# Flamingo gated block: values by seven block products, the output projection in one slot, another order at the end

## The chip, the cores and the metric

The kernel runs on one core of one Trainium2 chip. The metric is the device time of one execution in microseconds; three runs were timed, and one more was recorded by the hardware profiler. The engines are called as in the profile: PE is TensorE's matmul stream and PEld its weight loads, DVE is VectorE, ACT ScalarE, POOL GpSimd, SP the queue that issues most DMAs.

## The reference, cut to what matters

There are 8 batches of 512 rows (channels) by 2048 columns (positions). The row-wise layernorm of x gives queries and keys, the context gives values; attention runs inside windows of 128 positions with 8 heads of 32; the result goes through a GELU and an output projection and is added to x with a gate. Then a second layernorm feeds a router of 64 experts per row, whose eight best weights scale the row and mix rows of a bias table.

```python
q = einsum('ed,bdw->bew', Wq, qp) + bq        # qp: layernorm(x), windows of 128
k = einsum('ed,bdw->bew', Wk, qp) + bk
val = einsum('ed,bdw->bew', Wv, vp) + bv      # vp: context, 512 rows in, 256 out
attn = softmax(where(mask > 0, q·k / sqrt(32), -1e9))
o = gelu(attn · val)
x = x + tanh(g_xattn) * (Wo · o + bo) * mask
h = layernorm(x)                              # over the 2048 positions
s = softmax(h · router_weight.T + router_bias)   # 64 experts per row
w = the 8 largest of s per row, 0 elsewhere
x = x + tanh(g_ffn) * (h * sum(w) + w · expert_bias)
```

## The kernel before, in words

All arithmetic is in float32. The positions of a batch are cut in 4 chunks of 512, 32 chunks in all, and a chunk in two pairs of windows. The unit of the main loop (line 755) is one pair, called a slot here: slot `g` belongs to chunk `ch = g // 2`, and is even or odd. Eight slots make a batch; `fin` (line 774) counts them 0 to 7 from the second batch on, because the router of a batch is finished while the next batch runs.

The program is scheduled by hand (line 89): each engine executes its instructions in the order in which the code issues them, and a later instruction waits behind an earlier one that waits. The code's order is therefore the order of each engine's queue.

A slot issues, in this order: `scores` (line 430, query times key for 2 windows and 8 heads in four PSUM banks of the tag `sc`), `weigh` and `weighed` of the pair two slots back (lines 499 and 516, attention times values, emptied by ACT), `maxima` (line 456), `exps` in four quarters on ACT (line 461), `divide` by the row sums in two halves (line 473, DVE reciprocal and POOL multiplication), and between these the eight transposes of the pair before in four `turn`s (line 483, emptied by `turned` on ACT). `queries_and_keys` (line 361) projects half of the next chunk's queries and keys by seven block products of the Strassen-Winograd kind instead of eight; the sums of x blocks it needs come from `sums_of_x` (line 298) on POOL, its additions u4 and q from POOL, the others from DVE. `between(i)` puts turns between the products.

Values: `values` (line 409) computes a pair's values with the context window as stationary operand and 256 columns of `wv_sb` as moving operand, four blocks of 128 rows accumulated; `values_out` (line 420) adds the bias. In the loop each slot makes the values of the next chunk's pair of the same parity.

Output projection: `attend` (line 535) makes 128 of 512 rows for a chunk, with DVE adding the bias and multiplying by the mask, and POOL adding the result to x. Of a chunk's four attends, two (m = 0, 1) are issued at the end of an odd slot (line 928) and two (m = 2, 3) early in the following even slot (line 817). Even slots then transpose the new x (`turn_x`, line 560), odd slots make the router's logits of it (`logits`, line 568).

Router: in slot fin 2 the second layernorm's statistics are aggregated (line 888), in fin 3 the logits are gathered and `choose`d (lines 593, 605), in fin 4 `select` (line 630) finds the eight best, and from then on each slot scales two x blocks (`scale_x`, line 665, POOL) and adds the mix of expert rows (`mix`, line 676: two PE products, two DVE additions, one DMA out). In fin 5 the next batch's first layernorm is aggregated, and its chunk is normed by ACT (line 874).

PSUM has eight banks: four of `sc`, two of `tr` (transposes and `weigh`, line 87) and two of `mm` (all other products, line 88), each tag taken in turn. A product waits until the reader of the tile two before it in its tag is done.

The last two pairs and the end are written out (lines 943 to 1050): attention, values and attends of the last chunks, then the last logits, the expert choice and 8 scalings and mixes.

Of the kernel before, what the change touches and what calls it, by code (L numbers as in the profile page):

```python
# [35 lines left out]
def flamingo_gated_kernel(  # L36
# [81 lines left out]
    def load_mask(ch):  # L118
        t = work.tile([P, CW], F32, tag="mk", name=f"mk_{ch}", bufs=4)
        nc.sync.dma_start(t, masks[ch // NCH, :, columns(ch)].to_broadcast([P, CW]))  # L120
        mks[ch] = t
# [66 lines left out]
    ones = const.tile([P, P], F32, name="ones")  # L188
    nc.vector.memset(ones, 1.0)
# [126 lines left out]
    def mask(ch):  # L316
        m01 = work.tile([P, CW], F32, tag="m01", name=f"m01_{ch}", bufs=1)
        nc.vector.tensor_scalar(m01, mks[ch], 0.0, scale, ALU.is_gt, ALU.mult)
        mneg = work.tile([P, CW], BF16, tag="mneg", name=f"mneg_{ch}")
        nc.vector.tensor_scalar(mneg, m01, 0.0, None, ALU.is_equal)  # L320
        m01s[ch], mnegs[ch] = m01, mneg
        qss[ch] = work.tile([P, NE, CW], F32, tag="qs", name=f"qs_{ch}")
        kss[ch] = work.tile([P, NE, CW], F32, tag="ks", name=f"ks_{ch}")
# [12 lines left out]
    def first_queries_and_keys():  # L336


        parts = [(w, e, product([P, CW], f"pf_{i}_{e}", NE * i + e))
# [21 lines left out]
    def queries_and_keys(ch, e, between):  # L361


        es = slice(e * P, (e + 1) * P)
        x_, t_ = xn[ch], xts[ch]
        q, k = qss[ch][:, e, :], kss[ch][:, e, :]
        bq_, bk_, m01 = bq_sb[:, e : e + 1], bk_sb[:, e : e + 1], m01s[ch]
# [37 lines left out]
        nc.vector.tensor_tensor(k, k, m01, ALU.mult)  # L405
# [14 lines left out]
    def values_out(ch, h):  # L420
# [4 lines left out]
        vTs[ch, h] = vT  # L425

# [89 lines left out]
    def weighed(g):  # L516
        ch, hf = g // NH, g % NH
        if hf == 0:
            os_[ch] = work.tile([P, NE, CW], F32, tag="o", name=f"o_{ch}")
# [15 lines left out]
    def attend(ch, m, cs=whole, r=None):  # L535
# [12 lines left out]
        nc.gpsimd.tensor_tensor(xc, t[:, cs], xc, ALU.add)  # L548
# [116 lines left out]
    def scale_x(b, k, on_act=False):  # L665
        t = experts[b]
        j, mp = k // 2, k % 2
        for m in (2 * mp, 2 * mp + 1):
            xc = xr[b * NCH + j][:, m, :]
            a, d = t["a"][:, m : m + 1], t["d"][:, m : m + 1]  # L670
            if on_act:
                nc.scalar.activation(xc, xc, AF.Identity, bias=d, scale=a)
            else:
                nc.gpsimd.tensor_scalar(xc, xc, a, d, ALU.mult, ALU.add)  # L674

    def mix(b, k):
# [10 lines left out]
        for i in range(2):  # L687
            xc = xr[ch][:, 2 * mp + i, :]
            nc.vector.tensor_tensor(xc, pb[i], xc, ALU.add)  # L689
# [54 lines left out]
    def router_sums():  # L744
        pr = ps_tr.tile([P, E], F32, tag="tr", name="pr")
# [9 lines left out]
    for g in range(NG - NH):  # L755
# [7 lines left out]
        n_pieces = [4, 4, 4, 2, 2][g] if g < 5 else PER  # L763
# [4 lines left out]
        xch = ch - 2 if even and ch >= 2 else None  # L768
        lch = ch - 2 if not even and ch >= 2 else None
        pch = ch - 1 if not even and ch >= 1 else None  # L770

        vals = [] if (nxt, h) == (1, 0) or nxt == last else [(nxt, h)]
# [11 lines left out]


        if even:
            if nxt > 1:
                load_cx(nxt, 1)
            if nxt < last and nxt + 1 >= NCH:
                load_xn(nxt + 1)  # L790
        elif nxt < last:
            load_cx(nxt + 1, 0)
        if even and NCH <= ch - 1:
            load_xr(ch - 1)
# [8 lines left out]

        def read_x(n):

            for b, i in pieces[:n]:
                stats_x(b, i)
                if queue:
                    load_raw(*queue.pop(0))
            del pieces[:n]  # L810

# [3 lines left out]
        if even:  # L815
            if xch is not None:
                for m in (2, 3):
                    attend(xch, m)
                del os_[xch], mks[xch]
            exps(g, 1)  # L820
            exps(g, 2)
            mask(nxt)
            turn_(0)
            turn_(1)
            exps(g, 3)
# [3 lines left out]
            divide(g, 0)  # L829
            if g == 0:  # L830
                load_mask(2)
        else:
            exps(g, 1)
            if lch is not None:
                logits(lch)
                logits_out(lch)
# [12 lines left out]
        def between(i):  # L849
            if even:  # L850
                turn_x_(i)
# [6 lines left out]
            else:  # L858
                turn_(2)
                if pch is not None and nxt < last:  # L860
                    load_mask(nxt + 1)

        queries_and_keys(nxt, h, between)
        if fin == 5 and b4 + 2 < B:
# [5 lines left out]
        divide(g, 1)  # L870
        if not even and nxt < last:

            if (nxt + 1) % NCH == 0:
                norm(nxt + 1)
            sums_of_x(nxt + 1, 0)


        if fin == 4:
            select(b4)
        def stats():  # L880
            if even and xch is not None:
                for m in range(NM):
                    statistics2(xch, m)
            read_x(len(pieces))

        if fin != 4:
            stats()
        if fin == 2:
            aggregate(st2.pop(b4), NCH, f"2_{b4}")


        if even:
            turn_x_(2)
            for c_, h_ in vals:
                values(c_, h_, 0, 0)
                turn_(2)
                values(c_, h_, 1)
            if not vals:
                turn_(2)
            if nxt < last and (nxt + 1) % NCH:  # L900
                norm(nxt + 1, (0, 1))
            for c_, h_ in vals:
                values_out(c_, h_)
            if fin == 4:
                stats()
            turn_x_(3)
# [3 lines left out]
            if nxt < last and (nxt + 1) % NCH:  # L910
                norm(nxt + 1, (2, 3))
            if fin == 4:
# [5 lines left out]
        else:  # L918
# [5 lines left out]
            for c_, h_ in vals:  # L924
                values(c_, h_, 0, 0)
                values(c_, h_, 1)
                values_out(c_, h_)
            if pch is not None:
                for m in (0, 1):
                    attend(pch, m, r=m + 1)  # L930
# [6 lines left out]
        if g == 3:  # L937
            nc.gpsimd.tensor_scalar_mul(eb_sb, eb_sb, tgates[:, 1:2])
        for k in steps:
            mix(mb, k)  # L940


    z, b, h0 = last, B - 1, NG - NH
    load_xr(z - 1)
    scores(h0)
# [5 lines left out]
    for m in (2, 3):  # L951
        attend(z - 2, m)
    for k in (2, 3):
        scale_x(b - 1, k)
    exps(h0, 1)
    divide(h0, 0)
    turn(h0 - 1, 0)
    turned(h0 - 1, 0)
    values(z, 0, 0)
    turn(h0 - 1, 1)  # L960
    turned(h0 - 1, 1)
    values(z, 0, 1)
    values_out(z, 0)
    exps(h0, 2)
    exps(h0, 3)
    divide(h0, 1)
    turn_x(z - 2, 0)
    values(z, 1, 0)
    turn_x(z - 2, 1)
    values(z, 1, 1)  # L970
    values_out(z, 1)
    for m in range(NM):
        statistics2(z - 2, m)
    turn(h0 - 1, 2)
    turned(h0 - 1, 2)
    turn_x(z - 2, 2)
    mix(b - 1, 2)
    turn(h0 - 1, 3)
    turned(h0 - 1, 3)
    turn_x(z - 2, 3)  # L980
    mix(b - 1, 3)
    load_xr(z)

    g = h0 + 1
    scores(g)
    weigh(g - 2)
    weighed(g - 2)
    maxima(g, (0, 1))
    maxima(g, (2, 3))
    logits(z - 2)  # L990
    logits_out(z - 2)
    exps(g, 0)
# [3 lines left out]
    exps(g, 1)  # L996
# [4 lines left out]
    exps(g, 2)  # L1001
    for k in (4, 5, 6, 7):
        scale_x(b - 1, k)
    mix(b - 1, 4)
    weigh(g - 1)
    weighed(g - 1)
    exps(g, 3)
    divide(g, 1)
# [3 lines left out]
    gelu(z - 1)  # L1012
    mix(b - 1, 5)
# [3 lines left out]
    late += [0, 1, 2, 3, None, None]  # L1017
# [3 lines left out]
    mix(b - 1, 6)  # L1021
    for m in range(NM):
        attend(z - 1, m)
    mix(b - 1, 7)
    for k in range(KC):
        attend(z, k)
        turn_x(z - 1, k)

    table_of_exps()
    logits(z - 1)  # L1030
    logits_out(z - 1)
    for m in range(NM):
        statistics2(z - 1, m)
        statistics2(z, m)
    for k in range(KC):
        turn_x(z, k)
    aggregate(st2.pop(b), NCH, f"2_{b}")
    logits(z)
    logits_out(z)
    nmean, rs = refine(f"2_{b}")  # L1040
    experts[b] = {"nmean": nmean, "rs": rs}
    gather(b)
    choose(b)
    choose_exps(b)
    select(b)
    turn_weights(b)
    for k in range(2 * NCH):
        scale_x(b, k, k % 2 == 0)
    for k in range(2 * NCH):
        mix(b, k)  # L1050

# [33 lines left out]
```

## Time and profile before

| what | value |
|---|---|
| median of 3 runs | 1371.4 us (1369.75 to 1372.12) |
| the profiled execution's own time | 1372.72 us |
| its span, first to last instruction | 1370.9 us |
| mean granted PE clock | 0.985 |
| starts of `scores` at slots 14, 15, 16 | 306.62, 326.54, 346.53 us |
| starts of `scores` at slots 19 and 20 (fin 3 and 4) | 406.37 and 427.62 us |
| POOL, `divide` (L477), x128 | 1.909 us each |
| POOL, 128x512 additions (L548, L306 to L311) | 1.27 to 1.30 us each |
| ACT, `turned` (L497), x256 | 0.623 us each |

A row of the groups gives line, engine, operation, output and inputs, count, busy time and mean duration, then the idle time before it with what ended it. PE instructions are pipelined, so their pace is read from the starts of successive rows in the timeline and not from their durations. A float32 product appears as two instructions.

### The profile page before, as it was taken

The numbers are of one execution on the slowest core, as the hardware profiler recorded it, in microseconds if no ns is written. First come the engines' busy times: TensorE is split into PE (matmuls) and PEld (weight loads), VectorE is DVE, ScalarE is ACT, GpSimd is POOL, SyncE is SP. The second block draws the span as 40 slices with busy tenths as digits, with TensorE's granted clock in tenths as the row PEclk, the third lists the DMA queues.
The fourth block names the chain that finished last, engine by engine and source line by source line (L and its number), as shares of the span: only waits on it lengthen the run. The fifth ranks groups of instructions, "written<-read, shape, count | busy, mean of one in ns | idle before, by whom it ended". The sixth has DMA issues, their size and how long they took to land.

```text
span 1370.9 us, 26555 instructions
## 1 busy us (share of the span) xinstructions
PE 1317.3 (96%) x9816; PEld 961.0 (70%) x9816; DVE 912.9 (67%) x1981; ACT 832.0 (61%) x2837; POOL 778.0 (57%) x656
## 2 busy tenths in 40 slices
PE   7899999999999999999999999999999999999984
PEld 4686777777777677767777777776777777776642
DVE  5556665676676766786667767677677766567536
ACT  0565666757656666747665675666675566575533
POOL 3456565555566655557555566655556665556452
PEclk9999999999999999999999999999999999999997
DMA  8432323424434433444442444343444343232213
GB/s 276 133 102 71 101 65 129 131 70 156 153 131 139 161 100 133 147 140 141 151 137 96 146 162 141 129 158 97 139 147 161 109 131 105 75 122 78 104 67 123
DMA packets 109666, 173.32 MB, mean 126 GB/s; under 512 B 9185, under 2 KB 43617, under 8 KB 109409
## 3 DMA queue, kind: packets, MB, share of 16 engines
q1 hardware_dynamic: 105680, 168.32, 37.5%
q10 hardware_dynamic: 3856, 3.32, 0.7%
q8 instruction: 77, 1.26, 0.4%
q14 instruction: 53, 0.43, 0.1%
HBM read 138.06 MB, written 33.55 MB: 125 GB/s over the span
## 4 chain that ended last, share of the span: by engine, by line
PE 84%; DVE 11%; POOL 2%; DMA 1%; issue 1%; ACT 0%; DVEq 0%; POOLq 0%; ACTq 0%
PE qk L378 27%; PE po L539 16%; PE pv L415 13%; PE pt L491 7%; PE pl L574 4%; PE pb L685 4%; PE pa L510 4%; PE sc L447 3%; PE px L563 3%; DVE st L558 3%; DVE st L264 2%; PE sc L438 1%; PE pf L344 1%; DMA cx<-in_ctx 1%; DVE ks L405 1%
## 5 line engine op out<-in xcount | busy, mean ns | idle before, releaser
L477 POOL TENSOR_TENSOR at<-at,rsum 128x1024 f32<-128x1024 f32 x128 | 244.3, 1909 | 289.9 <-DVE rsum L476 255.4
L468 ACT ACTIVATE at<-sc,nmx 128x128 f32<-128x128 f32 x1024 | 365.7, 415 | 16.1 <-DVE nmx L459 16.1
L468 ACT ACTIVATION_READ_ACCUMULATOR at<-sc,nmx 128x1 f32 x1024 | 260.1, 254 | 0.0
L415 PE MATMUL pv<-wv_sb,cx 128*128 128x256 f32 x1024 | 242.6, 386 | 10.2 <-DMA cx<-in_ctx 10.2
L539 PE MATMUL po<-o,wo_sb 128*128 128x512 f32 x512 | 233.8, 599 | 0.0
L415 PEld LDWEIGHTS pv<-wv_sb,cx 128*128 128x128 f32 x1024 | 191.4, 194 | 33.8 <-DMA cx<-in_ctx 10.6
L548 POOL TENSOR_TENSOR xr<-t,xr 128x512 f32<-128x512 f32 x128 | 165.9, 1296 | 79.9 <-DVE t L545 79.5
L497 ACT COPY atT<-pt 128x512 f32<-128x512 f32 x256 | 151.1, 623 | 60.4 <-PE pt L491 60.3
L520 ACT COPY o<-pa 128x512 f32<-128x512 f32 x64 | 37.6, 587 | 243.9 <-PE pa L510 243.9
L459 DVE TENSOR_REDUCE nmx<-sc 128x4 f32<-128x512 f32 x256 | 158.7, 681 | 16.7 <-PE sc L447 16.6
L545 DVE SCALAR_TENSOR_TENSOR t<-po,bo_sb,mk 128x512 f32<-128x512 f32 x128 | 96.1, 751 | 109.5 <-PE po L539 104.6
L491 PEld LDWEIGHTS pt<-ident,at 128*128 128x128 f32 x1024 | 123.3, 142 | 61.8 <-issue 41.5
L539 PEld LDWEIGHTS po<-o,wo_sb 128*128 128x128 f32 x512 | 94.3, 190 | 100.4 <-issue 93.9
L565 ACT COPY x1T<-px 128x512 f32<-128x512 f32 x128 | 74.9, 587 | 139.3 <-PE px L563 136.2
L491 PE MATMUL pt<-ident,at 128*128 128x128 f32 x1024 | 152.2, 277 | 5.8 <-POOL at L477 5.3
L378 PE MATMUL qk<-xt,wq_sb 128*128 128x256 f32 x496 | 129.6, 384 | 4.0 <-DVE u L386 3.9
L378 PE MATMUL qk<-xn,ws 128*128 128x256 f32 x496 | 128.6, 382 | 0.0
L378 PE MATMUL qk<-xn,wk_sb 128*128 128x256 f32 x496 | 127.5, 380 | 0.0
L689 DVE TENSOR_TENSOR xr<-pb,xr 128x512 f32<-128x512 f32 x128 | 81.8, 683 | 36.4 <-PE pb L685 33.4
L674 POOL TENSOR_SCALAR xr<-xr,xa,xd 128x512 f32<-128x512 f32 x120 | 94.4, 798 | 18.6 <-DVE xa L650 18.6
L378 PEld LDWEIGHTS qk<-xn,ws 128*128 128x128 f32 x496 | 94.7, 191 | 13.0
L378 PEld LDWEIGHTS qk<-xn,wk_sb 128*128 128x128 f32 x496 | 89.4, 190 | 9.7
(108 smaller groups left out, 2016.3 us busy)
## 6 DMA issues: line engine op xcount, KB each, us to landing
out_dram<-xr SPq DMA_DIRECT2D x64, 512.0 KB, 3.4
cx<-in_ctx SPq DMA_DIRECT2D x63, 512.0 KB, 5.2
raw<-in_x SPq DMA_DIRECT2D x112, 256.0 KB, 3.4
xn<-in_x SPq DMA_DIRECT2D x28, 1024.0 KB, 7.3
xr<-in_x SPq DMA_DIRECT2D x28, 1024.0 KB, 7.8
mk<-in_mask_Bx1x_ff SPq DMA_DIRECT2D x32, 256.0 KB, 5.3
xr<-in_x SPq DMA_DIRECT2D x8, 256.0 KB, 6.4
xr<-in_x ACTq DMA_DIRECT2D x8, 256.0 KB, 6.9
```

The lines of the kernel that those rows point to most:

```text
L378: nc.tensor.matmul(out_, w_[:, j, es], xb[:, j, :], start=(j == 0), stop=(j == NM // 2 - 1))
L415: nc.tensor.matmul(pv[:, i, :], cx[:, m, i * W : (i + 1) * W], wv_sb[:, m, :], start=(m == 0), stop=(m == NM - 1),)
L459: nc.vector.tensor_reduce(p["nmx"][:, r, :, :], p["sc"][r], AX.X, ALU.max, negate=True)
L468: nc.scalar.activation(p["at"][i][:, h, :], p["sc"][r][:, i, e, :], AF.Exp, bias=p["nmx"][:, r, i, e : e + 1], accum_out=p["rsum"][:, i, h ...
L477: (engine or nc.gpsimd).tensor_tensor(p["at"][i], p["at"][i], rs[:, :, None].to_broadcast([P, H, W]), ALU.mult)
L491: nc.tensor.transpose(pt[:, r, :], p["at"][i][:, e * HR + r, :], ident)
L497: nc.scalar.copy(p["atT"][i][:, e * HR : (e + 1) * HR, :], p.pop("pt"))
L539: nc.tensor.matmul(po[:, cs], wo_sb[:, e, m * P : (m + 1) * P], os_[ch][:, e, cs], start=(e == 0), stop=(e == NE - 1),)
L545: nc.vector.scalar_tensor_tensor(t[:, cs], po[:, cs], bo_sb[:, m : m + 1], mks[ch][:, cs], ALU.add, ALU.mult)
L548: nc.gpsimd.tensor_tensor(xc, t[:, cs], xc, ALU.add)
L674: nc.gpsimd.tensor_scalar(xc, xc, a, d, ALU.mult, ALU.add)
L689: nc.vector.tensor_tensor(xc, pb[i], xc, ALU.add)
```

## The change

- **Values by seven products.** For chunks 2 to 31 `values_by_seven` replaces `values`: in the even slot of the chunk itself, seven block products with 128 moving columns, in the four `sc` banks. `sums_of_c` makes three sums of context blocks on POOL in the slot's middle, a fourth comes between the products; `sums_of_wv` makes four sums of weights once, in the fourth slot. DVE empties seven products instead of two. Both halves of a chunk's context are loaded in the odd slot before.
- **Output projection.** All four attends of a chunk are issued at the end of the odd slot, the first two in banks sc0 and sc1. The logits of an odd slot are those of the chunk whose x was turned in the even slot before, with its statistics behind them (not in fin 3; there they come in fin 2, after the values).
- **Order in the slots.** In even slots the turns 0 and 1 follow `weigh` directly; `exps` 3 and `mask` move between the products; `divide` 0 follows the projections and `divide` 1 the values; reading raw x pieces moves to the slot's end. The first five slots read 2, 2, 4, 4, 4 pieces instead of 4, 4, 4, 2, 2. The mask's load moves to the even slot's start, with 3 buffers instead of 4; tag `o` has 1 buffer.
- **The end.** Scores of the last pair are issued between the last values' products; the last divide runs on DVE; the last chunk's attends add on DVE; scalings and mixes 4 to 7 of the batch before move behind the last logits; the last scalings are split over DVE, POOL and ACT, and four of the last additions go to POOL, with ACT emptying PSUM for them.

```diff
+    def sums_of_c(ch):
+        a11, a21, a22 = cxs[ch, 0][:, d1, :], cxs[ch, 1][:, d1, :], cxs[ch, 1][:, d2, :]
...
+        nc.gpsimd.tensor_tensor(t1, a21, a22, ALU.add)
+        nc.gpsimd.tensor_tensor(t2, t1, a11, ALU.subtract)
+        nc.gpsimd.tensor_tensor(a21, a11, a21, ALU.subtract)
+
+    def values_by_seven(ch, between, banks=range(4)):
...
+        def pair(*ops):
+            pv = product([P, len(ops), NPP, P], f"pv_{ch}_{len(banks)}", banks.pop(0))
+            for n, (a, w_) in enumerate(ops):
+                for i in range(NPP):
+                    for j in range(NM // 2):
+                        nc.tensor.matmul(
+                            pv[:, n, i, :], a[:, j, i * W : (i + 1) * W], w_[:, j, :],
+                            start=(j == 0), stop=(j == NM // 2 - 1),
+                        )
+            return [pv[:, n, :, :] for n in range(len(ops))]
+
+        bias = [bv_sb[:, None, e].to_broadcast([P, NPP, P]) for e in (e1, e2)]
+        p1, p6 = pair((c0[:, d1, :], v11), (t2, wt2))
+        nc.vector.tensor_tensor(s1, p1, bias[0], ALU.add)
+        nc.vector.tensor_tensor(u2, p6, s1, ALU.add)
+
+        nc.gpsimd.tensor_tensor(t2, c0[:, d2, :], t2, ALU.subtract)
+        between(0)
+        p2, p5 = pair((c0[:, d2, :], v21), (t1, v12))
+        nc.vector.tensor_tensor(vt[0][:, :, e1], p2, s1, ALU.add)
+        nc.vector.tensor_tensor(s5, p5, bias[1], ALU.add)
+        nc.gpsimd.tensor_tensor(u4, u2, s5, ALU.add)
+        between(1)
+        p7, p3 = pair((c1_[:, d1, :], wt3), (t2, v22))
...
+        nc.vector.tensor_tensor(u3, p7, u2, ALU.add)
+        nc.vector.tensor_tensor(vt[0][:, :, e2], p3, u4, ALU.add)
+        nc.gpsimd.tensor_tensor(vt[1][:, :, e2], u3, s5, ALU.add)
+        between(2)
+        (p4,) = pair((c1_[:, d2, :], wt4))
+        nc.vector.tensor_tensor(vt[1][:, :, e1], p4, u3, ALU.add)
...
         exps(g, 0)
         if even:
-            if xch is not None:
-                for m in (2, 3):
-                    attend(xch, m)
-                del os_[xch], mks[xch]
+            turn_(0)
+            turn_(1)
             exps(g, 1)
             exps(g, 2)
-            mask(nxt)
-            turn_(0)
-            turn_(1)
-            exps(g, 3)
+            if vch is not None:
+                sums_of_c(vch)
             if fin != 4:
                 for k in steps:
                     scale_x(mb, k)
-            divide(g, 0)
...
+            if xch is not None:
+                logits(xch)
+                logits_out(xch)
+                if fin != 3:
+                    for m in range(NM):
+                        statistics2(xch, m)
...
         queries_and_keys(nxt, h, between)
+        if even:
+            divide(g, 0)
...
+            if vch is not None:
+                values_by_seven(vch, between_values)
...
+            divide(g, 1)
+            if fin == 2:
+                for m in range(NM):
+                    statistics2(xch, m)
+                aggregate(st2.pop(b4), NCH, f"2_{b4}")
             if fin == 4:
                 turn_weights(b4)
             turn_(3)
             if nxt < last and (nxt + 1) % NCH:
                 norm(nxt + 1, (2, 3))
+            read_x(len(pieces))
...
         if g == 3:
             nc.gpsimd.tensor_scalar_mul(eb_sb, eb_sb, tgates[:, 1:2])
+            sums_of_wv()
         for k in steps:
             mix(mb, k)
+        if pch is not None:
+            for m in range(NM):
+                attend(pch, m, r=m if m < 2 else None)
+            del os_[pch], mks[pch]
```

## The prediction

> **What bounds the kernel now.** I read the page first (engine shares, chain, groups by shape), then the waits of TensorE in the loop, then the timelines of single slots. One turn of the main loop is a slot; two slots, even and odd, serve one chunk, eight serve a batch, and I count them 0 to 7 by the code's `fin`.
>
> ```profile
> PE 1317.3 (96%) x9816; PEld 961.0 (70%) x9816; DVE 912.9 (67%) x1981; ACT 832.0 (61%) x2837; POOL 778.0 (57%) x656
> ...
> PE 84%; DVE 11%; POOL 2%; DMA 1%; issue 1%; ACT 0%; DVEq 0%; POOLq 0%; ACTq 0%
> PE qk L378 27%; PE po L539 16%; PE pv L415 13%; PE pt L491 7%; PE pl L574 4%; PE pb L685 4%; PE pa L510 4%; PE sc L447 3%; PE px L563 3%; DVE st L558 3%; DVE st L264 2%; PE sc L438 1%; PE pf L344 1%; DMA cx<-in_ctx 1%; DVE ks L405 1%
> ```
>
> The chain that ended last is TensorE work. Its waits between 100 and 1270 us say how little it stands still; the largest:
>
> ```profile
> PE pl L574 <- DVE xr L689: 3.6, 11, 0.3
> PE sc L438 <- DVE t L545: 2.6, 5, 0.5
> PE px L563 <- POOL xr L548: 2.5, 2, 1.4
> ```
>
> A chunk takes 39.9 us (scores start at 306.62, 326.54, 346.53) and TensorE has no gap in it. So whatever is taken from TensorE is won, and any new wait of TensorE is lost in full. The first line names a wait to remember: the logits product takes the PSUM bank from which VectorE still adds the expert mix.
>
> **The skill.** "TensorE: Matmul & The Clock Gate", LDWEIGHTS section: a load costs its columns over 1.2 GHz, about 107 ns for 128, and fp32 has no fast load. The trace agrees: products with 64 moving columns come every 0.112 us (rows L747). The same page, HAM oscillation: an idle TensorE is put on half clock. The trace shows it after less idle time than the page names (below). "SBUF — State Buffer", Who interferes with whom: a VectorE `tensor_scalar` and a GpSimd instruction hold a shared port for a whole instruction. L320 takes 1.30 us in the mean against 0.43 at 46.64 us, where GpSimd is quiet. It agrees.
>
> **The change, part by part.**
>
> ```profile
> 320.62 1.89 PE L415 MATMUL pv<-wv_sb,cx 128*128 128x256 f32 x8
> 322.35 0.60 PE L491 MATMUL pt<-ident,at 128*128 128x128 f32 x4
> 322.78 1.89 PE L415 MATMUL pv<-wv_sb,cx 128*128 128x256 f32 x8
> ```
>
> (1) Values. From start to start, eight instructions of 256 columns take 1.73 us (0.216 each), four transposes, 128 weights and 128 columns, 0.43 (0.109). A chunk now has 32 of the first: 6.92 us. After it has 7 products x 2 windows x 2 blocks x 2 passes = 56 of 128 columns. No row has this shape as an ordinary fp32 product; the nearest are 0.109 (transposes) and 0.112 (L747, where the load sets the pace), the slowest relative 0.126 (four L447 side by side). I take 0.111: 6.2 us, so -0.7 a chunk, 30 chunks: **-21** (-25 to +4).
>
> (2) The even slot loses its two attends between `weigh` and the turns. The second turn then needs the PSUM buffer that ScalarE is still emptying. The kernel's third slot, at 71 us, has no attends and so this order already; the third line is the usual pace:
>
> ```profile
> 73.36 1.43 PE L491 MATMUL pt<-ident,at 128*128 128x128 f32 x8
> 74.14 0.42 PEld L491 LDWEIGHTS pt<-ident,at 128*128 128x128 f32 x4 [0.35 <-ACT o L520]
> ...
> 312.38 1.04 PE L491 MATMUL pt<-ident,at 128*128 128x128 f32 x8
> ```
>
> The second turn starts 0.34 us late. 29 even slots: **+10**.
>
> (3) GpSimd gets 3 sums of 1.24, one of 1.26 and two of 0.73 a chunk, 6.4 us on 24 (60% to 76%), and all four attend additions come in a row, ahead of these. I follow its queue. In the odd slot its second divide starts at 12.99 (339.53 - 326.54), then 1.86, four sums of x 4.95, four additions 4.95: 24.8, with the even slot starting at 20.1, so 4.7 into it. Three sums of c (3.7), two scalings (1.5), about 0.3 for VectorE's mask on the shared port, u4 (0.73): 11.0. Behind u4 VectorE writes k, q, k x mask and the reciprocal (1.6), GpSimd divides (1.9) and makes t2 anew (1.3): 15.85. TensorE wants t2 at 15.65 (scores 1.22, weigh 1.02, turns 1.2, seven products 6.05, two turns of x 0.87, then 1.77 + 0.44 + 1.77 + 0.44 + 0.87). So **+0.2** a chunk (0 to +0.9), 29 times: **+6**. The cover is gone: anything later on GpSimd shows.
>
> (4) VectorE gets seven emptyings of about 0.42 for two of 0.68: +1.6 us a chunk, on 26.5. Regular slots hold that. Slot 2 of a batch does not. Now its statistics lie under the values' matmuls, and still the mix additions are just late:
>
> ```profile
> 408.23 1.27 DVE L689 TENSOR_TENSOR xr<-pb,xr 128x512 f32<-128x512 f32 x2
> ...
> 408.96 1.94 PE L574 MATMUL pl<-x1T,rw_sb 128*64 128x512 f32 x8 [0.30 <-DVE xr L689]
> ```
>
> Afterwards all of it follows the last value product: emptying 0.42, reciprocal 0.12, four statistics 2.37, aggregate 0.83, two raw pieces 1.19, refine 0.83, first addition 0.6, 0.15 of latency: 6.5 us. TensorE meanwhile has a turn 0.44, mix 1.06, scores 1.22, weigh 1.02: 3.7. So the logits of slot 3 wait **2.8**. Behind them queue all turns and projections of that slot.
>
> (5) Slot 4's scalings come behind a divide that now follows the values, so the mix additions, maxima and, in slot 5, the statistics (2.37, moved here) and aggregate (0.83) push VectorE's u2 behind the turn after which TensorE wants its bank: 0.8 at the logits and about 1.2 at the fifth product, **+2.0** (0.7 to 2.6). In slot 5 the norm (four of 0.73 on ScalarE) starts only after the reciprocal, so GpSimd's row of (3) begins 3 us later: slot 6 waits for the additions and for t2, 1.0 to 3.2, taken **+2.5**.
>
> (6) Waits of this length cost again:
>
> ```profile
> 58.82 1.13 PE L378 MATMUL qk<-xt,wq_sb 128*128 128x256 f32 x4 [2.28 <-DVE u L386]
> 59.79 1.52 PE L378 MATMUL qk<-xn,ws 128*128 128x256 f32 x4
> 61.10 1.06 PE L491 MATMUL pt<-ident,at 128*128 128x128 f32 x4
> 61.96 1.84 PE L378 MATMUL qk<-xt,wq_sb 128*128 128x256 f32 x4
> ```
>
> After 2.28 us idle, four products take 1.67 instead of 0.86 for 3.4 us: 1.7 lost. After 1.66 idle (46 us) they did not. I take one such a batch, **+1.7** (0 to 3.4).
>
> A batch so costs 2.8 + 2.0 + 2.5 + 1.7 = 9.0, less the 0.8 that slots 3 and 5 wait or stretch now: +8.2. Seven batches, of which the first and last have about half: 6 x 8.2 = **+49** (22 to 67).
>
> (7) Head, slots counted from the kernel's start. The first two read fewer raw pieces, and their waits of 1.66 and 2.28 and the half clock go: -5. At the end of the fourth, GpSimd scales `eb` (5.4) and makes four sums of wv (2.9) ahead of all four additions: these end 14.3 us into the fifth, where TensorE wants them at 7.3, so 7.0 + 1 (t2) + 3 (clock), against 4.6 lost there now: +7. Together **+2** (-3 to +6).
>
> (8) End. Before, the last scores but one start at 1274.65 and the last logits at 1339.33: 64.7. Afterwards I walk 55: waits of about 5 where ScalarE's exponentials hold the two turn buffers, but divide on VectorE removes the 4.53 us wait at 1312 (behind eight scalings, 6.0), and mixes and scalings move into the expert selection. Two attends (3.5) move ahead of it, so -6. From the last logits on: statistics no longer delay the last sum (-1.8), four mix additions (+1.1) come before the selection and four after it (+2.6), against earlier warm mixes and adds shared out (-3): -1. **-7** (-12 to -2).
>
> (9) At nothing: the mask load waits for the last attend (0.9 into the even slot) and lands 5.3 later, 6.2, before VectorE's 7.6; SP's x and xr loads queue behind it by 0.9 and are used a slot later. Both c loads go out a slot ahead (5.2 to land). Uncovered, each delay would add to (3).
>
> Sum: -21 + 10 + 6 + 49 + 2 - 7 = **+39**. On the profiled execution's 1372.7: 1411.7; the median lies 1.3 below it, so **1410**, slower.
>
> **Rivals.** A, faster: VectorE and GpSimd absorb (3) to (6), as they do now with 67% and 57%; then -21 + 10 - 7 = -18: 1353. For it speaks that TensorE has almost no waits today; against it, 0.30 us at L574, which shows that the slack is used up. It decides if a batch loses under about 3 us. B, the change doesn't do what it says: at 0.126 or more per product, the values save nothing: +25, 1435. Against it, the two nearest rows. C: GpSimd is late by 0.9 in every even slot, +20: 1430. D: only the wait of (4) and half of (5): 1374 to 1385.
>
> **Chances.** Forecast (1385 to 1426) 0.50, A 0.23, no change (within 0.2%, about what a measurement of this kernel can tell) 0.05, D 0.10, B and C 0.12. Slower 0.72, same 0.05, faster 0.23. The range 1357 to 1438 leaves out half of A and the outer part of B and C; the forecast's own is 1385 to 1426.
>
> **What would show it.** Value products 0.111 apart; a 0.34 us wait for L520's successor in even slots; slot 3 lengthened by about 3 us with the logits waiting for VectorE; slot 6 by about 2 waiting for GpSimd; more half-clock stretches. If slot 3 is not over 22 us, (4) is wrong and A likely.

## The result, and the profile after

The changed kernel takes **1440.15 us** (median of 4 runs, 1436.85 to 1444.24) against 1371.67 (4 runs) in the same measurement: ratio 1.050, 95% interval 1.047 to 1.054. Slower, as predicted, but by 68 us instead of 39; 1440.15 lies 14 us beyond the forecast's own 1385 to 1426, and 2 beyond 1438, the upper end of the whole range. The profiled execution took 1437.97, its span 1436.2, which is 65.3 over the span before.

First the page of the changed kernel: busy time by engine, then the chain that ended last.

```profile
PE 1322.2 (92%) x10536; PEld 978.2 (68%) x10536; DVE 965.0 (67%) x2134; ACT 832.5 (58%) x2842; POOL 968.4 (67%) x837
...
PE 53%; POOL 20%; DVE 16%; issue 4%; ACT 4%; DMA 3%; POOLq 0%; SPq 0%; DVEq 0%; ACTq 0%
PE qk L381 17%; PE po L619 8%; PE pv L477 8%; POOL xr L628 5%; PE pt L569 5%; PE pl L654 3%; POOL at L555 3%; DVE st L638 3%; PE pa L588 2%; PE pb L766 2%; POOL xr L755 2%; PE sc L525 2%; PE px L643 2%; ACT xn L283 2%; POOL cx L456 1%
```

TensorE is as busy as before (1322 against 1317), only 65 us more spread out. The chain has passed from TensorE, 84%, to TensorE 53% with GpSimd 20% and VectorE 16%. Which waits made it pass, the list of TensorE's waits over the whole span says (waited for, us in total, times, longest):

```profile
PE pl L654 <- DVE xr L774: 25.5, 13, 3.3
PE pv L477 <- POOL cs L488: 15.9, 14, 1.6
...
PE qk L381 <- DVE u L389: 9.3, 9, 1.3
PE pt L569 <- ACT o L600: 8.3, 31, 3.1
PE pb L766 <- DVE ks L403: 6.6, 6, 1.1
PE px L643 <- POOL xr L628: 5.1, 5, 2.0
PE pb L766 <- DVE xr L774: 4.7, 4, 2.7
```

The first was 3.6 in all before. From start to start of the scores, slot by slot: a regular even slot went from 19.92 to 19.63 us, a regular odd one from 19.99 to 20.31; slot 3 of a batch from 21.25 to 24.55 or 26.18, slot 4 from 20.56 to 20.93, slot 5 from 20.41 to 24.11, slot 6 from 19.92 to 21.49. So the regular chunk costs the same as before, and nearly all is lost in slots 3 to 6.

By stretches of the span. Some work has changed its stretch: chunk 4's values have moved out of the first and chunk 28's into the third, and two attends from the last stretch into the first.

| stretch | before | after | difference |
|---|---|---|---|
| slots 0 to 7 | 144.8 | 149.3 | +4.5 |
| slots 8 to 55 | 971.1 | 1025.6 | +54.6 |
| slots 56 to 61 | 118.3 | 128.7 | +10.4 |
| slot 62 to the end | 96.3 | 90.8 | -5.5 |

Slot 0 itself starts 1.3 later, at 41.8 us. TensorE waits longer for the first loads there (13.0 against 10.2 in all), and this varies: in the runs below slot 0 starts between 38.7 and 41.6.

The worst wait, in slot 3, first VectorE, then TensorE:

```profile
759.37 0.19 DVE L554 RECIPROCAL rsum<-rsum 128x8 f32<-128x8 f32 x1
759.48 2.42 DVE L638 BATCH_NORM_STATS2 st<-xr 128x6 f32<-128x512 f32 x4
761.81 0.61 DVE L242 BATCH_NORM_AGGREGATE mv<-st 128x2 f32<-128x24 f32 x4
...
762.54 1.28 DVE L262 BATCH_NORM_STATS2 st<-raw 128x6 f32<-128x512 f32 x2
...
765.25 1.27 DVE L774 TENSOR_TENSOR xr<-pb,xr 128x512 f32<-128x512 f32 x2
```

```profile
761.63 1.08 PE L588 MATMUL pa<-atT,vT 128*32 128x128 f32 x32
765.98 1.94 PE L654 MATMUL pl<-x1T,rw_sb 128*64 128x512 f32 x8 [3.27 <-DVE xr L774]
```

Statistics, aggregate, raw pieces and refinement all stand between the last value's emptying (759.03) and the mix additions (765.25), and the logits product needs the bank that the first addition frees. VectorE is not busy beyond its means: before 759 it had stood idle for 3.3 us, waiting for value products.

### The profile page after: what moved, and what is told of

It is laid out like the page before. It is cut to its first block, busy times and chain, and to the rows that moved or that the text cites. A ratio compares the mean times of both kernels' runs of the same rounds, so it can differ in the third digit from the quotient of the medians.

```text
span 1436.2 us, 28486 instructions
## 1 busy us (share of the span) xinstructions
PE 1322.2 (92%) x10536; PEld 978.2 (68%) x10536; DVE 965.0 (67%) x2134; ACT 832.5 (58%) x2842; POOL 968.4 (67%) x837
## 3 DMA queue, kind: packets, MB, share of 16 engines
q8 instruction: 83, 1.36, 0.4%
## 4 chain that ended last, share of the span: by engine, by line
PE 53%; POOL 20%; DVE 16%; issue 4%; ACT 4%; DMA 3%; POOLq 0%; SPq 0%; DVEq 0%; ACTq 0%
PE qk L381 17%; PE po L619 8%; PE pv L477 8%; POOL xr L628 5%; PE pt L569 5%; PE pl L654 3%; POOL at L555 3%; DVE st L638 3%; PE pa L588 2%; PE pb L766 2%; POOL xr L755 2%; PE sc L525 2%; PE px L643 2%; ACT xn L283 2%; POOL cx L456 1%
## 5 line engine op out<-in xcount | busy, mean ns | idle before, releaser
L546 ACT ACTIVATION_READ_ACCUMULATOR at<-sc,nmx 128x1 f32 x1024 | 264.5, 258 | 0.0
L619 PE MATMUL po<-o,wo_sb 128*128 128x512 f32 x512 | 228.4, 598 | 1.5 <-ACT o L613 1.4
L569 PE MATMUL pt<-ident,at 128*128 128x128 f32 x1024 | 159.8, 280 | 11.4 <-ACT o L600 8.3
L628 POOL TENSOR_TENSOR xr<-t,xr 128x512 f32<-128x512 f32 x124 | 154.1, 1275 | 15.1 <-DVE t L625 15.1
L569 PEld LDWEIGHTS pt<-ident,at 128*128 128x128 f32 x1024 | 119.0, 142 | 63.8 <-issue 31.3
L381 PEld LDWEIGHTS qk<-xt,wq_sb 128*128 128x128 f32 x496 | 85.6, 192 | 18.2 <-DVE u L389 11.5
L283 ACT ACTIVATE xn<-xn,nmr,rs 128x512 f32<-128x512 f32 x112 | 84.4, 808 | 23.3 <-DVE nmr L275 23.3
```

The lines of the kernel that those rows point to most:

```text
L283: e.activation(xn[ch][:, m, :], source[:, m, :], AF.Identity, bias=nmrs[ch // NCH][:, m : m + 1], scale=rs[:, m : m + 1],)
L381: nc.tensor.matmul(out_, w_[:, j, es], xb[:, j, :], start=(j == 0), stop=(j == NM // 2 - 1))
L546: nc.scalar.activation(p["at"][i][:, h, :], p["sc"][r][:, i, e, :], AF.Exp, bias=p["nmx"][:, r, i, e : e + 1], accum_out=p["rsum"][:, i, h ...
L569: nc.tensor.transpose(pt[:, r, :], p["at"][i][:, e * HR + r, :], ident)
L619: nc.tensor.matmul(po[:, cs], wo_sb[:, e, m * P : (m + 1) * P], os_[ch][:, e, cs], start=(e == 0), stop=(e == NE - 1),)
L628: (engine or nc.gpsimd).tensor_tensor(xc, t[:, cs], xc, ALU.add)
```

## The experiments

Two theories. **Order**: TensorE waits for items that stand behind others on VectorE and GpSimd, and the same work in another order costs nothing. **Load**: with seven products the two engines have too much to do, and a wait mended in one place comes back in another. Each verdict is against runs of the kernel before on the same chip.

**The values, plain again, everything else as changed.**

```
-            if vch is not None:
-                sums_of_c(vch)
...
-                values_by_seven(vch, between_values)
+                for i_ in range(NH):
+                    values(vch, i_, 0, i_)
+                    between_values(i_)
+                    values(vch, i_, 1)
+                    values_out(vch, i_)
+                between_values(2)
...
-            sums_of_wv()
```

> The changed kernel with the plain values (32 products of 256 columns a chunk, two emptyings) at the same place in the even slot, and without the sums of context and weights; all else, with the order of statistics and attends, stays. If the order of the queues costs (my theory): the products cost 0.7 us a chunk more (+21), the waits for t2 go (0.7 + 1.6 a batch, -15), the logits still wait about 3.3 us in slot 3 of a batch: 1446, between 1435 and 1455. If the additional VectorE and GpSimd work of the seven products is the cause, the waits go with it: about 1385, and below 1410.

Measured: 1427.54, ratio 1.042 (1.041 to 1.044), between both. The regular even slot is 20.29, so the seven products save 0.66 there; but without them slot 5 is 1.5 us shorter, slot 6 waits for nothing and the fifth slot of the head waits 2.0 instead of 4.8 for GpSimd. In this order the seven products cost 12.6 net by the medians, 11 by the ratios. And without them and their sums the change still loses 57 us: the greater part of the loss belongs to the order of the other work. Slot 3 waits 3.1 as before.

**The last statistics of a batch ahead of the values.**

```
         if fin == 4:
             select(b4)
+        if fin == 2:
+            for m in range(NM):
+                statistics2(xch, m)
+            aggregate(st2.pop(b4), NCH, f"2_{b4}")
...
             divide(g, 1)
-            if fin == 2:
-                for m in range(NM):
-                    statistics2(xch, m)
-                aggregate(st2.pop(b4), NCH, f"2_{b4}")
```

> The changed kernel with the four statistics and the aggregate of slot 2 of a batch ahead of the values' products instead of behind them. Same work on every engine. Order theory: the logits of slot 3 wait under 0.7 us instead of 3.27, and the half clock that follows in most batches goes: seven times 3 to 5 us, 1415 (1407 to 1424). If the load is the cause, the work only moves the wait elsewhere: 1433 or more.

Measured: 1431.7, ratio 1.045 (1.044 to 1.047), a miss for the order theory by 8 us and close to what the load theory says. Slot 3's wait fell to between 0.72 and 0.99, which is nearly the 0.7 of the order theory; but slot 2 grew by 2.2. The timeline of GpSimd, then of TensorE, in slot 2:

```profile
753.02 1.03 POOL L244 TENSOR_TENSOR rs<-v,half 128x4 f32<-128x4 f32 x1 [1.17 <-DVE v L243]
754.02 1.26 POOL L488 TENSOR_TENSOR cs<-cx,cs 128x512 f32<-128x512 f32 x1
```

```profile
755.34 1.16 PE L477 MATMUL pv<-wv_sb,cs 128*128 128x128 f32 x8 [1.93 <-POOL cs L488]
```

The aggregate ends with a power on GpSimd. Moved forward it stands ahead of t2 and waits for VectorE, with t2 behind it. That looks like load and is order again: the edit moved one instruction too many. (In the second attempt below, with the aggregate behind u4, slot 2 has no such wait.)

**The odd slots' statistics into the even slots, ahead of the values** (those of slot 4 into slots 7 and 1, two each).

```
-                if fin != 3:
+                if ch == NC - 2:
                     for m in range(NM):
                         statistics2(xch, m)
...
+        if even and xch is not None and fin not in (2, 4):
+            for m in range(NM):
+                statistics2(xch, m)
...
```

> The changed kernel with the second layernorm's statistics out of the odd slots (where they stand ahead of the projections): into the even slots ahead of the values; those of slot 4 of a batch, two each, behind the projections of slots 7 and 1. Slot 2 is left as in the change. Order theory: in slot 5 the waits of 1.28 (projection for VectorE) and 1.09 (mix for k) fall to 0.3 together, and regular odd slots lose 0.2 to 0.3 us: 1423 (1416 to 1430). Load theory: even slots grow by what odd ones lose: 1435 or more.

Measured: 1424.22, ratio 1.040 (1.038 to 1.041), as the order theory says. Slot 5 went from 24.11 to 21.77: the wait of the fifth product for u2 is gone, and that of the mix for k fell from 1.09 to 0.29. Slot 3 kept its 3.28, slot 6 its 1.6. The 0.2 to 0.3 us that regular odd slots were to lose did not come: they stay at 20.31.

**All mended at once, first attempt**: both edits above, the even slot's first divide behind t2, its second turn behind the first projections, slot 4's scalings inside the values, and the head as told below under "The head alone".

> The changed kernel with every order mended that its trace names: statistics of slot 2 and of odd slots moved as in the two kernels before, the even slot's first divide behind the making of t2, the second turn between the projections, slot 4's scalings ahead of the last value product, and in the head the ones set before the raw pieces are read and the weights' sums and the scaling of the expert table in GpSimd's idle stretch. Work and shapes are unchanged. Order theory: TensorE's waits of 9.5 us a batch fall under 2.5 and the half clock with them, the head gains 6: 1368 (1355 to 1385). Load theory: above 1400.

Measured: 1417.01, ratio 1.035 (1.033 to 1.036): missed by 32 us at the least, as the load theory says. The regular even slot fell to 19.24, so the turn no longer waits. But three new waits had come. The one in slot 7 (24.5 us in most batches, in place of 20.3), on VectorE, GpSimd and TensorE:

```profile
656.78 0.42 DVE L486 TENSOR_TENSOR vu<-pv,vs 128x256 f32<-128x256 f32 x1
657.12 0.19 DVE L554 RECIPROCAL rsum<-rsum 128x8 f32<-128x8 f32 x1
...
660.01 0.42 DVE L498 TENSOR_TENSOR vT<-pv,vu 128x256 f32<-128x256 f32 x1 [1.74 <-POOL vu L493]
```

```profile
657.40 1.90 POOL L555 TENSOR_TENSOR at<-at,rsum 128x1024 f32<-128x1024 f32 x1 [3.90 <-DVE rsum L554]
659.25 0.72 POOL L493 TENSOR_TENSOR vu<-vu,vs 128x256 f32<-128x256 f32 x1
```

```profile
660.49 0.70 PE L516 MATMUL sc<-mneg,negw 32*128 32x512 bf16 x2 [1.97 <-DVE vT L498]
```

With the divide I had moved its reciprocal too, which now stood behind four statistics and two emptyings. GpSimd idles 3.9 us for a reciprocal of 0.19, u4 comes late behind the divide, and the next scores wait for the bank that u4's user empties. By its time alone this run speaks for the load theory. An engine that idles 3.9 us ahead of the late item speaks against it.

**All mended, second attempt**: as the first, with the reciprocal directly behind the projections and only GpSimd's multiplication behind t2; the aggregate issued after u4; the turned weights in bank 0 in place of 1; and in slot 2 the mix ahead of the raw pieces and the refinement.

```
+        elif even:
+            inverse(g, 0)
...
                 elif i == 1:
                     turn_x_(2)
+                    if fin == 2:
+                        aggregate(st2.pop(b4), NCH, f"2_{b4}")
...
         for k in steps:
             mix(mb, k)
+        if fin == 2:
+            read_x(len(pieces))
+            nmean, rs = refine(f"2_{b4}")
```

> As e8_all, with the four places mended where e8's TensorE still waits: in even slots VectorE's reciprocal of the first divide stands directly behind the projections and only GpSimd's multiplication behind t2; the last statistics of a batch are aggregated after u4, so GpSimd's power no longer stands ahead of t2; the turned weights use the bank that is emptied first; in slot 2 of a batch the mix additions stand ahead of the raw pieces and of the refinement. Order-of-queues theory (the waits come from what stands ahead on VectorE and GpSimd, not from how much they do): e8's 2.25 and half clock in slot 2, 0.9 in slot 4, 2.0 and half clock in slot 7 go, about 8 a batch, so 1365 (1355 to 1385), level with or faster than the kernel before. Load theory (the two engines have too much to do in this arrangement, a wait mended here comes back there): above 1400.

Measured: **1358.66**, ratio 0.992 (0.990 to 0.994). The same operations as in the changed kernel, in another order (and one in another PSUM bank), are 81 us faster and pass the kernel before. VectorE and GpSimd are as busy as in the changed kernel (970.4 and 968.2 us against 965.0 and 968.4). The load theory, which said above 1400, has fallen.

**The same with plain values.**

> As e10_all2, with the plain value products (32 of 256 columns a chunk, no sums of c) in the same place and order. It prices the seven products where nothing waits for them. Order-of-queues theory: an even slot grows by 0.66 for 32 x 0.216 in place of 56 x 0.111, so 30 chunks give +20 over e10_all2, 1385 (1375 to 1395). Load theory: GpSimd gets 6.4 us less a chunk, so this is as fast as e10_all2 or faster.

Measured: 1362.32, ratio 0.994 (0.992 to 0.996): only 3.7 more, neither expectation. Even slots are 0.66 longer, as foreseen, but slot 7 is 20.31 instead of 21.77: with seven products the order still had a wait of 0.77 at the scores of slot 7.

**That wait removed**: the scalings of even slots behind the divide, where GpSimd idles, instead of ahead of the projections' u4.

```
                     if vch is not None:
                         divide(g, 0, inverted=True)
+                    if fin is not None:
+                        for k in steps:
+                            scale_x(mb, k)
```

> As e10_all2, with GpSimd's two scalings of even slots behind the divide of the values' stretch, where GpSimd idles 2 us, instead of ahead of the projections' u4. In e10's slot 6 VectorE waits 3 us for that u4, all after it comes later, and the next scores wait 0.78 for the last value's bank with TensorE at half clock after it: slot 7 is 21.77 instead of 20.31. Order-of-queues theory: slot 7 falls to 20.3 and slots 3 and 5 by some tenths: 1349 (1345 to 1353). Load theory (the wait is VectorE's amount of work, not where u4 stands): no change from e10_all2, 1357 to 1361.

Measured: 1351.68, ratio 0.985 (0.983 to 0.987). Slot 7 is 20.31. The time is what the order theory says, though slots 3 and 5 did not shorten. Slot 6 without this edit (the second attempt), first GpSimd's making of t2, then VectorE:

```profile
630.30 1.27 POOL L488 TENSOR_TENSOR cs<-cx,cs 128x512 f32<-128x512 f32 x1
```

```profile
629.69 0.48 DVE L403 SCALAR_TENSOR_TENSOR ks<-qk,bk_sb,u 128x256 f32<-128x256 f32 x1 [2.97 <-POOL u L395]
630.09 0.41 DVE L407 TENSOR_TENSOR qs<-qk,u 128x256 f32<-128x256 f32 x1
630.42 1.70 DVE L408 TENSOR_TENSOR ks<-ks,m 128x512 f32<-128x512 f32 x1
```

and with it:

```profile
627.12 1.54 POOL L488 TENSOR_TENSOR cs<-cx,cs 128x512 f32<-128x512 f32 x1 [0.36 <-PE pv L477]
```

```profile
626.12 0.48 DVE L403 SCALAR_TENSOR_TENSOR ks<-qk,bk_sb,u 128x256 f32<-128x256 f32 x1 [1.45 <-POOL u L395]
626.52 0.42 DVE L407 TENSOR_TENSOR qs<-qk,u 128x256 f32<-128x256 f32 x1
626.85 0.68 DVE L408 TENSOR_TENSOR ks<-ks,m 128x512 f32<-128x512 f32 x1
```

VectorE's wait for u4 halves, and its multiplication by the mask falls from 1.70 to 0.68. Without the edit it starts 0.12 behind GpSimd's making of t2; with it, 0.27 ahead, and then it is GpSimd that takes longer, 1.54 instead of 1.27.

**The end's last mixes shared out** (on top of the last one): four scalings of the final mixes on VectorE instead of GpSimd.

```
-    by_vector, by_gpsimd = ((0, 0),), ((1, 0), (2, 0), (3, 0), (4, 0), (5, 0), (6, 0))
+    by_vector = ((0, 0), (3, 0), (4, 0), (5, 0), (6, 0))
+    by_gpsimd = ((1, 0), (2, 0))
```

> As e14_scale_behind, with the first scalings of the last four shared mixes on VectorE instead of GpSimd. In the last mixes GpSimd takes 2.04 for an addition and a scaling while VectorE idles 1.3, and TensorE waits for the buffers. If GpSimd sets the pace there: 1.27 to 1.4 a mix, so 2 to 3 us less than e14_scale_behind. Rival (the output stores or ScalarE's copies and scalings, 1.4 a mix, set the end): under 1 us less.

Measured: **1348.93** (1347.05 to 1350.71), ratio 0.984 (0.982 to 0.985), the fastest of all: 2.7 less than without the edit, though the two kernels' runs overlap. What the edit did is seen in the last mixes, VectorE's additions one mix apart, without the edit and with it:

```profile
1341.44 0.69 DVE L779 TENSOR_TENSOR xr<-pb,xr 128x512 f32<-128x512 f32 x1 [1.29 <-POOL xr L760]
1343.43 0.69 DVE L779 TENSOR_TENSOR xr<-pb,xr 128x512 f32<-128x512 f32 x1 [1.30 <-POOL xr L760]
```

```profile
1339.55 0.69 DVE L779 TENSOR_TENSOR xr<-pb,xr 128x512 f32<-128x512 f32 x1
...
1340.97 2.48 DVE L779 TENSOR_TENSOR xr<-pb,xr 128x512 f32<-128x512 f32 x4
```

A mix takes 1.42 instead of 1.99, so four of them save 2.3. The page of the fastest kernel:

```profile
PE 1302.5 (97%) x10536; PEld 973.6 (72%) x10536; DVE 969.5 (72%) x2138; ACT 830.8 (62%) x2842; POOL 965.5 (72%) x833
...
PE 75%; DVE 12%; POOL 8%; ACT 2%; DMA 2%; issue 2%; DVEq 0%; POOLq 0%; ACTq 0%
```

Beside the page of the changed kernel: VectorE 969.5 against 965.0 us, GpSimd 965.5 against 968.4. Nearly the same load, and 88 us less span.

**And this one with plain values**, the price of seven products where little waits:

> As e15_end_shared, with the plain value products in the same place (32 of 256 columns a chunk, no sums of c). It prices the seven products in an arrangement in which the loop waits under 0.6 us a batch. If they are worth what they take from TensorE: 0.66 in each of 30 even slots, +20, less 0.35 in each slot 5, so 1366 (1362 to 1370). If the sums of c cost on GpSimd and VectorE about what the products save, as between e10_all2 and e11_all2_plain (3.7): 1351 to 1355.

Measured: 1360.2, ratio 0.993 (0.991 to 0.995). The seven products are worth 11.3 us by the medians, 12.6 by the ratios. That lies between the expectations: 0.66 in even slots, but slots 3 and 5 are 0.4 and 0.35 longer with them. In slot 3 the projections wait 0.35 for the logits' emptying on VectorE, 0.12 with plain values. In slot 5 the loss stands at the start: from the first scores to `weigh` it takes 1.56 instead of 1.22. The scores take the four `sc` banks, and VectorE empties the last value product there only 0.31 after they have started (594.50 against 594.19); that this is the cause is read from the trace and not tested.

**The head alone**, three edits on the changed kernel: `ones` set ahead of the raw pieces, `sums_of_wv()` in slot 3 and the scaling of `eb` in slot 7 ahead of GpSimd's first divide.

> As the changed kernel, with three things of the head undone: the ones are set ahead of the raw pieces, the four sums of wv stand in slot 3 and the scaling of the expert biases in slot 7, each ahead of GpSimd's first divide where it idles. Order-of-queues theory: the waits of 2.2 and half clock in slot 1 and of 4.8 in slot 4 go, and nothing after slot 8 changes: 8 to 11 us less, 1430 (1427 to 1433). Rival (the head's waits come from the fewer raw pieces and the missing attends): no change, over 1436.

Measured: 1429.26, ratio 1.042 (1.041 to 1.044), as the order theory says. From slot 0 to slot 8 it takes 136.5 instead of 149.3; the loop after it keeps its waits. What `ones` did in the changed kernel:

```profile
65.71 1.03 PE L418 MATMUL pv<-wv_sb,cx 128*128 128x256 f32 x4
68.90 4.86 PE L834 MATMUL pr<-rw_sb,ones 128*128 128x64 f32 x32 [2.17 <-issue]
```

On VectorE the memset stands behind an emptying and two raw pieces and starts at 68.63; the router's sums wait for it. Their 32 products then take 4.79 us from start to start of the next row, against 3.61 in the mended head, and the granted clock is 0.75 over them and 0.58 in the 5.3 us that follow.

**The kernel before, with only its very last divide on VectorE**, a part of the change.

```
-    divide(g, 1)
+    divide(g, 1, nc.vector)
```

> The kernel before, with only the very last divide on VectorE as in the changed kernel. GpSimd does eight scalings (6.0) ahead of it there, and TensorE's turn waits 4.53 at 1312 with half clock after it. If that wait is on the path, as the prediction's eighth term says: 4 to 6 us less, ratio 0.9955 to 0.997. Rival (VectorE's mix additions then stand ahead, or the time is taken back at the last logits): no change.

Measured: 1364.62, ratio 0.995 (0.994 to 0.997). This wait of the kernel before is gone:

```profile
1312.21 1.97 PE L491 MATMUL pt<-ident,at 128*128 128x128 f32 x8 [4.53 <-POOL at L477]
```

The end takes 89.8 instead of 96.3 from slot 62 on. That is more than the whole new end gained (-5.5), with one word.

**Two misses.** On the second attempt, the odd slot's mix behind the attends instead of ahead of them:

> As e10_all2, with the expert mix of odd slots behind the four attends instead of ahead of them. The odd slot has been 20.31 us in every version so far against 19.99 before, without a wait of TensorE. If that comes from a 64-row product followed by 128-row ones (neighbours), the place of the mix ahead of the scores takes it away again: odd slot about 20.15, 2 to 5 us less than e10_all2. If it comes from the attends themselves: no change. If VectorE's mix additions get late behind four attend outputs: waits in the next even slot, 1 us a chunk, 1390.

Measured: 1370.35, ratio 1.000 (0.999 to 1.001). The odd slot grew to 20.95. The four mix products take 1.97 instead of the 1.06 that they take elsewhere ahead of the scores, and the list of TensorE's weight loads gives the reason, the banks of the last two attends:

```profile
PEld pb L771 <- DVE t L630: 15.5, 25, 0.6
```

And the scalings and mixes 4 to 7 of the last batch but one moved from behind the last logits to ahead of the last statistics:

> As e10_all2, with the scalings 4 to 7 and the mixes 4 to 7 of the last batch but one moved ahead of the last chunk's transposes and statistics, instead of behind the last logits. The time from the last logits to the end was 31.6 before and 35.5 after the change. Order-of-queues theory: what stands in the queues between the last logits and the final adds goes, 3 to 6 us less than e10_all2. Rival (VectorE's additions only move ahead of the attends and statistics that the last logits wait for): no change or up to 3 more.

Measured: 1360.42, ratio 0.993 (0.991 to 0.996), 1.8 more than the second attempt. From slot 62 on the profiled executions differ by 2.6 (93.0 against 90.4), to the rival's side.

## Why the prediction was right in sign and too small

**Term 1, values: right.** The new products come every 0.111 us; from start to start, eight take 0.89:

```profile
882.27 1.05 PE L477 MATMUL pv<-wv_sb,cx 128*128 128x128 f32 x8
883.16 1.06 PE L477 MATMUL pv<-wt,cs 128*128 128x128 f32 x8
```

**Term 2, the second turn: right**, 0.17 of wait and 0.17 of a later restart in each even slot; it went when the turn was moved, in the first attempt (19.63 to 19.24).

**Term 3, t2: right in GpSimd's queue, wrong in where it shows.** Regular even slots have no wait for t2, so nothing of its +6 lies there; slots 4 and 6 wait 0.72 and 1.6.

**Terms 4 to 6, right in kind.** Slot 3 waits 3.27 (predicted 2.8), with half clock after it in four of the six batches from slot 16 on (predicted: one such stretch in every batch). Slot 6 lengthened by 1.6 (predicted 2.5).

The error, by stretches: 65.3 was measured and 39 predicted.

- **The loop, some 14 us short.** From slot 8 to 55 the sum gives about +41, measured +54.6. Half of it is in the odd slots, 0.32 each, 7.7 in 24: I costed the attends' move at nothing on TensorE. The trace shows no wait there; the mix now stands between a turn and the attends, and from its start to theirs takes 1.20 where it took 1.06 ahead of the scores. The two fences below show it, the kernel before and then the run with early statistics, whose odd slots are those of the change. With the turn, turn to attends is 1.73 against 1.50 for both; the rest is that eight attend products (3.53) came for 16 value products (3.45). The other half is the balance of the batch terms, and what went wrong there is **term 5, slot 5**: I found the waits of 0.8 and 1.2 (measured 0.84 and 1.28), but did not follow VectorE's queue to its next reader. The mix product waits another 1.09 for the bank of k (third fence), and the slot grew by 3.7, not 2.0. Slot 6, 0.9 less than forecast, gives some of it back.

```profile
325.48 1.13 PE L685 MATMUL pb<-eb_sb,wT 64*128 64x512 f32 x4
326.54 0.39 PE L438 MATMUL sc<-mneg,negw 32*128 32x512 bf16 x4
```

```profile
729.17 1.27 PE L766 MATMUL pb<-eb_sb,wT 64*128 64x512 f32 x4
730.37 7.13 PE L619 MATMUL po<-o,wo_sb 128*128 128x512 f32 x16
```

```profile
816.72 1.13 PE L381 MATMUL qk<-xt,wq_sb 128*128 128x256 f32 x4 [1.28 <-DVE u L389]
...
821.55 1.02 PE L766 MATMUL pb<-eb_sb,wT 64*128 64x512 f32 x2 [1.09 <-DVE ks L403]
```

- **Term 7, the head, 6 short.** I costed the moved memset of `ones` at nothing. Against the mended head it lengthens slots 1 and 2 by 5.4. The waits of slot 4 cost 7.4 instead of the 11 walked. The waits of 1.66 and 2.28 are gone as predicted, but I did not see that others would take their place. One in slot 1, for GpSimd's divide, takes 3.6 back with the half clock after it (the four projection products that start at 55.59 take 1.71 instead of 0.86); in slot 3 TensorE waits 0.80 for VectorE and 1.36 for ScalarE.

```profile
53.57 0.66 PE L569 MATMUL pt<-ident,at 128*128 128x128 f32 x4 [1.94 <-POOL at L555]
```

- **Term 8, the end, 5 short.** The stretch to the last logits took 55.3 as walked (55). From there on it took 35.5 against 31.6 before, where I had taken 1 off. Two pairs of mix additions stand on VectorE, 2.47 us each, one inside the expert selection and one behind it. The selection ends only 0.5 later after the last logits than before (14.6 against 14.1), so most is lost behind it: the second pair, and the last mixes, on each of which GpSimd spends 2.04. There I had credited a gain for "adds shared out". This is the second attempt, whose end is that of the changed kernel:

```profile
1342.65 1.27 POOL L779 TENSOR_TENSOR xr<-pbs,xr 128x512 f32<-128x512 f32 x1
1343.91 0.77 POOL L760 TENSOR_SCALAR xr<-xr,xa,xd 128x512 f32<-128x512 f32 x1
1344.64 1.27 POOL L779 TENSOR_TENSOR xr<-pbs,xr 128x512 f32<-128x512 f32 x1
```

- Slots 56 to 61 came as summed: 6.2 for chunk 28's values, -1.4 for two chunks, 1.6 for terms 2 and 3, 4.1 for half a batch, 10.5; measured 10.4. The remaining 1.3 is the later start of slot 0.

The forecast's own step that failed is thus the sum's size: the attends' move and three terms (5, 7, 8) took an instruction or a successor at nothing, which made the loop 14, the head 6 and the end 5 us too short. The direction and the waits of slots 3, 5 and 6 were no luck. **Rival A**, that slack absorbs the waits, failed for this order and is true of another: 1349 with the same operations. That its 1353 lies so near is partly luck: it counts 10 for the second turn, which that order no longer has, and leaves out the odd slots' 0.32. B failed on 0.111. C's cost was not where it stood, but it named the right queue. D failed, since the waits of slot 6 and the half clock came too.

**Still open**: why the mix followed by attends takes 0.14 longer than followed by scores (no run isolates it; the one aimed at it hit a bank wait), and whether an edit removes the last 0.35 to 0.4 in slots 3 and 5. No run takes the attends' move back alone, so its 7.7 us are read from the traces and not from a run without it.

## What to carry to other kernels

When a change adds work to two engines that are each two thirds busy, look for what stands ahead of each item that TensorE waits for; 81 us lay here in order alone, at nearly unchanged busy time of both. A moved step is every instruction it issues, on every engine: the reciprocal behind a divide, the power behind an aggregate and a 0.17 us memset each cost more here than the step they belong to. And when an attempt to mend fails, look whether the late engine idled just before the late item: where it did, in the two attempts here that fell short of their forecast, it was the order again.

## What the runs showed of the hardware that was not expected

TensorE's half clock came after waits of 1.94, 1.97, 2.17 and 3.27 us, but not in every repetition of the same wait: after the 3.27 of slot 3 in four of six. After one of the four (logits at 936.93) the granted clock was 0.79 over 8 us, after one of the other two (logits at 765.98) 1.00; these slots took 26.18 and 24.54. The Trainium skill, "TensorE: Matmul & The Clock Gate", HAM oscillation, puts the limit at idle gaps above 3.4 us; all of these are shorter, and the measurement decides.

VectorE's multiplication of two operands from SBUF, 128x512, takes 1.70 us where it starts 0.12 behind a GpSimd `tensor_tensor`, and 0.68 where it starts 0.27 ahead of it (fences of the scalings' edit). The Trainium skill, "SBUF — State Buffer", Who interferes with whom, says that a VectorE instruction with two SBUF inputs contends with a GpSimd instruction that reads SBUF; the runs agree. The prediction had counted this only for VectorE's `tensor_scalar`, though the multiplication of k by the mask is such an instruction and stands ahead of every first divide.
